# A four-layer graph network on one core: turns between the halves of a product, sorted keys turned in fours, and q rows gathered beside p rows

## The chip, the cores and the metric

The kernel runs on one core of one Trainium2 chip. The metric is the device time of one execution in microseconds (us); the smaller the better. The kernel before takes 6629.94 us, the median of three runs (6616.99 to 6645.70). Beside the times there is one profiled execution with a hardware trace of every engine: TensorE (PE, with its weight loads as PEld), VectorE (DVE), ScalarE (ACT), GpSimd (POOL) and the queue of SyncE (SP).

## What is computed

A graph of 4096 nodes with 512 features and 65,536 edges, sorted by their destination, passes through four layers. Each layer normalizes the nodes, applies a ReLU, runs a graph layer and adds its result to the nodes.

```python
# layer 0: x = x + softmax over the features of an 8-head attention over the edges' distinct pairs
# layer 1: x = x + relu(sum over edges of d[row] * d[col] * h[col], times W1)
# layer 2, h = relu(layernorm(x)):
edge_feat = concatenate([h[src], h[dst], edge_attr], axis=-1)
m = mish(mish(edge_feat @ W1 + b1) @ W2 + b2)          # one message per edge
agg = segment_sum(m, dst, num_segments=4096)
u = mish(concatenate([h, agg], axis=-1) @ W3 + b3)
x = x + layernorm(h + u @ W4 + b4) * gamma + beta
# layer 3: x = x + relu(sum over edges of d[row] * d[col] * (h @ W.T + b)[row])
```

Here mish(x) is x * tanh(softplus(x)). In layer 2 the product of the edge features with W1 is split: p = h @ W1[:512] and q = h @ W1[512:1024] + b1 are made once for each node, kept in two tables in HBM, and an edge's first product is p[src] + q[dst] + edge_attr @ W1[1024:].

## The kernel before

Nodes lie in 32 blocks of 128. Edges are put in order by a sort inside the kernel, and then taken as tiles of 128 edges which all belong to one block of nodes; a tile's sum over its edges is a product with a one-hot matrix.

**The front.** Three pieces of work are written as Python generators and advanced in turn, one step each, by `Side(...).finish()`: `by_order(0)`, the sort of the edges by source node (wrapped in `faster`, which gives it three steps in two rounds); `project`, which makes W0's product for the 32 blocks; and `attributes`, which writes the edge attributes with the edge's ends into a table in HBM. PE, ACT, DVE and POOL execute their instructions in the order in which these steps issue them (`manual_schedule`). So an instruction that has to wait keeps back everything behind it on its engine, from whichever of the three it comes.

A block of `project` is four steps: DVE normalizes it (L547); PE turns it in four transposes into the PSUM tile tr and ACT copies it with a ReLU to h_t (`relu_t`, L424 and L426), and the block before is put away (L531 to L533); two of the four parts of the product (L557); the other two, and then the product for the attention scores (L564). An fp32 matmul of the source is two MATMUL instructions in the trace.

The sort works in place on DVE (L166, L167) and between some of its passes turns all keys with PE and ACT (L174, L176, L178). At its end it fetches each tile's sorted keys with a gather (L276), takes them apart on DVE, and `placed` turns them: five tiles of 128x128, each with one transpose (L288) and one copy by DVE (L289), and one PSUM tile for all. It runs three times for the order by source and once for the order by destination. The latter, `by_order(1)`, is advanced beside the edge loop of layer 1.

**The edge loop of layer 2** (`messages`) takes groups of U2 = 4 tiles, 132 groups in all. It is a software pipeline with the order of each engine written out: at iteration i the rows for group i+2 are fetched, group i+1 gets its attribute products, group i its first mish, group i-1 its second product, and group i-2 its second mish and its sums.

- `fetch_rows` gathers four times 128 rows of p into pg (L452), `add_rows` then gathers the rows of q with an add in the DMA onto the same pg (L1047); `fetch_ends` fetches the attributes and ends (L987). All these are issued by POOL.
- `turn_attributes` (L1061, copied by L1063), then `attribute_products` (L1071), which DVE adds to pg (L1148, L1158).
- The first mish is a Sigmoid, an Arctan and a Sin on ACT into qg (L1118, L1139, L1154), and a product of pg with it on DVE, for the tiles 0 and 1 (L1155) and 2 and 3 (L1163).
- `turn_h` turns a tile of h on PE (L1078) and ACT copies it (L1080). Tiles 0 and 1 of group i are turned at the end of iteration i, among the sums of group i-2; tiles 2 and 3 in iteration i+1 behind the first second product. All turns, with that of the attributes, share two PSUM buffers, tr_ps.
- `second_product` (L441) has two PSUM buffers, m_ps; DVE adds b2 into z (L1121, L1132, L1144, L1161).
- The second mish is on ACT (L1127, L1141, L1150) and DVE (L1152); `add_message` makes the sum of a tile (L1090), and DVE adds it to the block (L462). Attribute products and sums share four PSUM buffers, small_ps.

After the loop the rest of layer 2, and layer 3 with its own edge loop, follow; the change does not touch them.

## Time and profile before

| what | us |
|---|---|
| median of three runs | 6629.94 |
| lowest and highest run | 6616.99, 6645.70 |
| profiled execution, its time | 6629.94 |
| its span, first to last instruction | 6628.1 |
| edge loop of layer 2 | 2926, about 44% of the span |
| front up to the attention loop's first gather | 276 |
| PE busy with second products, L441 m_ps | 1913.9 |
| POOL issuing the adding gathers, L1047 (528 of them) | 939.1 |

The profiled execution is the median run itself; the 1.8 us between its time and its span lie outside the first and last instruction. A row of the timeline gives start, length, engine, line, operation, output and inputs, and how many instructions were merged; in brackets stands how long the engine was idle before the row and which instruction released it. A row's length counts the pipeline of the last matmul, so the starts of neighbouring rows tell more about PE's pace than the lengths. Busy shares over the whole span mix stages; what an edit costs has to be read in its own stage.

### The profile page before, as it was taken

To read this page: it belongs to the slowest core of one execution; us is meant where nothing else is said; L and a number is where in the kernel's file an instruction comes from. 1 tells how busy PE (TensorE), PEld (TensorE's weight loads), DVE (VectorE), ACT (ScalarE), POOL (GpSimd) and SP (SyncE) were. 2 spreads that over 40 slices of the span, in tenths; PEclk is the share of its full clock that TensorE was granted. 3 is DMA by queue.
4 is the path that set the end of the run, shared out by engine and by line. 5 is a ranking of instruction groups with operands and counts; after the bars stand their busy time and mean duration, and the time that the engine had idled before them with its cause. 6 is when DMAs were issued, how large, how long until landed. Compare 5 with 4: busy or idle time off the path is not lost. (4 is left out here: it accounts for less than half of the span.)

```text
span 6628.1 us, 64370 instructions
## 1 busy us (share of the span) xinstructions
PE 5750.5 (87%) x17918; PEld 2937.7 (44%) x17918; DVE 3882.4 (59%) x6892; ACT 3086.4 (47%) x4232; POOL 3658.3 (55%) x3326
## 2 busy tenths in 40 slices
PE   6577777779988789999999999999999999877777
PEld 4356555434443344444444444444444566422222
DVE  7466666836664456565656656565665456545555
ACT  3144444421100167777777777777777533200000
POOL 1255555136666488666676666666666111256665
PEclk9788888889999999999999999999999999977778
DMA  8655555457777555444545554444545211255665
GB/s 228 157 153 155 153 155 154 145 182 221 227 221 204 163 126 114 104 102 102 101 104 103 102 105 101 103 102 103 103 103 104 65 64 67 99 162 168 192 204 162
DMA packets 424655, 908.39 MB, mean 137 GB/s; under 512 B 135734, under 2 KB 135734, under 8 KB 424278
## 3 DMA queue, kind: packets, MB, share of 16 engines
q0 software_dynamic: 264768, 721.66, 43.9%
q1 hardware_dynamic: 159510, 182.40, 8.6%
q8 instruction: 152, 2.49, 0.2%
q14 instruction: 225, 1.84, 0.1%
HBM read 800.88 MB, written 102.94 MB: 136 GB/s over the span
## 5 line engine op out<-in xcount | busy, mean ns | idle before, releaser
L441 PE MATMUL m_ps<-w_sb,h_t 128*128 128x512 f32 x4224 | 1913.9, 596 | 0.2 <-issue 0.2
L846 PE MATMUL sum_ps<-g,oh 128*128 128x512 f32 x2144 | 1158.5, 676 | 272.9 <-DVE acc L462 145.2
L441 PEld LDWEIGHTS m_ps<-w_sb,h_t 128*128 128x128 f32 x4224 | 771.7, 190 | 921.7 <-issue 913.7
L1047 POOL DMA_INDIRECT pg<-qtab,eg x528 | 939.1, 1779 | 160.9 <-issue 158.2
L462 DVE TENSOR_TENSOR acc<-acc,sum_ps 128x512 f32 x800 | 550.1, 688 | 778.5 <-PE sum_ps L846 333.6
L452 POOL DMA_INDIRECT pg<-ptab,eg x528 | 518.5, 982 | 608.0 <-ACT h_t L1080 419.7
L760 PE MATMUL sum_ps<-rows,oh 128*128 128x261 f32 x2176 | 611.0, 435 | 271.8 <-issue 192.7
L846 PEld LDWEIGHTS sum_ps<-g,oh 128*128 128x128 f32 x2144 | 428.8, 212 | 942.8 <-issue 539.7
L452 POOL DMA_INDIRECT g<-ytab,s_dst x544 | 547.1, 1006 | 479.1 <-DMA x_mid<-x 199.1
L452 POOL DMA_INDIRECT rows<-htab,s_dst x544 | 519.9, 956 | 457.1 <-PE sum_ps L760 271.8
L452 POOL DMA_INDIRECT g<-ztab,d_src x528 | 515.9, 977 | 399.1 <-PE sum_ps L846 163.8
L760 PEld LDWEIGHTS sum_ps<-rows,oh 128*128 128x128 f32 x2176 | 445.4, 213 | 374.1 <-issue 208.5
L987 POOL DMA_INDIRECT eg<-aug,d_eid x528 | 508.5, 963 | 161.0 <-issue 159.2
L1080 ACT COPY h_t<-tr_ps 128x512 f32<-128x512 f32 x528 | 296.6, 588 | 562.1 <-PE tr_ps L1078 424.7
L1090 PE MATMUL small_ps<-z,oh 128*128 128x512 f32 x1056 | 533.9, 608 | 8.4 <-DVE z L1152 8.4
L1152 DVE TENSOR_TENSOR z<-z,t 128x1024 f32<-128x1024 f32 x264 | 311.9, 1223 | 207.6 <-issue 185.0
L462 DVE TENSOR_TENSOR acc<-acc,small_ps 128x512 f32 x528 | 362.7, 687 | 87.9 <-DVE acc L462 69.8
L1332 ACT ACTIVATE t_end<-acc,dis 128x512 f32<-128x512 f32 x32 | 23.0, 721 | 835.7 <-DMA g<-ztab,d_src 400.0
L1078 PEld LDWEIGHTS tr_ps<-ident,pg 128*128 128x128 f32 x2112 | 245.9, 141 | 288.0 <-issue 148.2
L1078 PE MATMUL tr_ps<-ident,pg 128*128 128x128 f32 x2112 | 299.5, 275 | 43.9 <-DVE pg L1155 39.6
L1144 DVE TENSOR_TENSOR z<-m_ps,b_bc 128x512 f32<-128x512 f32 x132 | 91.4, 693 | 390.5 <-PE m_ps L441 206.9
L1132 DVE TENSOR_TENSOR z<-m_ps,b_bc 128x512 f32<-128x512 f32 x132 | 91.4, 692 | 374.6 <-PE m_ps L441 371.1
(274 smaller groups left out, 8384.2 us busy)
## 6 DMA issues: line engine op xcount, KB each, us to landing
aug<-row SPq DMA_DIRECT2D x32, 560.0 KB
xt<-in_x_dram SPq DMA_DIRECT2D x16, 1024.0 KB
row<-in_edge_attr_dram SPq DMA_DIRECT2D x32, 512.0 KB
rows<-htab,s_dst POOLq DMA_INDIRECT x544
g<-ytab,s_dst POOLq DMA_INDIRECT x544
eg<-aug,d_eid POOLq DMA_INDIRECT x528
pg<-ptab,eg POOLq DMA_INDIRECT x528
pg<-qtab,eg POOLq DMA_INDIRECT x528
```

The source lines that it names most:

```text
L441: nc.tensor.matmul(ps, h_t[:, k, :], w_sb[:, k0 + k, :], start=start and k == 0, stop=stop and k == KC - 1)
L452: nc.gpsimd.indirect_dma_start(out=dst_ap, out_offset=None, in_=table, in_offset=bass.IndirectOffsetOnAxis(ap=idx, axis=0))
L462: nc.vector.tensor_add(into, into, ps)
L760: nc.tensor.matmul(ps[:, c, :HW], oh[:, j + k, :], rows[:, j + k, c * HW:(c + 1) * HW], start=k == 0, stop=k == 1)
L846: nc.tensor.matmul(ps, oh[:, j + k, :], g[:, j + k, :], start=k == 0, stop=k == pair - 1)
L987: nc.gpsimd.indirect_dma_start(out=eg[:, j // 2, (j % 2) * HALF:(j % 2 + 1) * HALF], out_offset=None, in_=aug.rearrange("e c -> (e c)").un ...
L1047: nc.gpsimd.indirect_dma_start(out=pg[:, j, :], out_offset=None, in_=qtab, in_offset=bass.IndirectOffsetOnAxis(ap=end_of(eg, j, 1), axis=0 ...
L1078: nc.tensor.transpose(h_ps[:, k, :], h[:, j, k * P:(k + 1) * P], ident)
L1080: nc.scalar.copy(h_t, h_ps)
L1090: nc.tensor.matmul(ps, oh, m, start=True, stop=True)
L1132: nc.vector.tensor_add(zz[:, 1, :], ps, b2_bc)
L1152: nc.vector.tensor_mul(mz[:, j:j + 2], mz[:, j:j + 2], t[:, j:j + 2])
```

## The change

It has three parts.

In `project` the normalizing moves into a generator `norms` that hands out blocks. A block's turn is issued between the first and the second half of the product of the block in front of it; before its own product come that second half and the score product.

In `placed` four tiles are turned into one PSUM tile and copied with one DVE instruction, then the fifth; a step ends between transposes and copy, and work of the other generators is issued there.

In the edge loop the rows of q are gathered into a tile of their own, qg, with three buffers, and DVE adds them to pg in two instructions. The same tile then takes the Sigmoid. Tiles 0 and 1 of a group are turned at the beginning of the next iteration, directly before its first second product, and no longer among the sums; the turn of the attributes follows directly on those of tiles 2 and 3; the attribute products come before the third second product and no longer after it; `fetch_ends` is issued before `fetch_rows`. DVE's product for tiles 2 and 3 moves behind the second sum.

```diff
         def placed(into, what):
-            for g in range(G):
-                n = min(P, TT - g * P)
-                ps = ppool.tile([P, P], F32, name="turn")
-                nc.tensor.transpose(ps, what[:, g, :], ident)
-                nc.vector.tensor_copy(into[:, g * P:g * P + n], ps[:, :n])
+            for g in range(0, G, 4):
+                n = min(4, G - g)
+                ps = ppool.tile([P, n, P], F32, name="turn")
+                for k in range(n):
+                    nc.tensor.transpose(ps[:, k, :], what[:, g + k, :], ident)
+                yield
+                cols = slice(g * P, min((g + n) * P, TT))
+                nc.vector.tensor_copy(into[:, cols], ps.rearrange("p g t -> p (g t)")[:, :cols.stop - cols.start])
...
-            placed(d_eid, val)
+            yield from placed(d_eid, val)
...
-                yield
-                h_t = relu_t(lp, lps, hn)
-                if waiting is not None:
-                    put_away(*waiting)
-                yield
-                ps = lps.tile([P, D], F32, name="wh_ps")
-                for k in range(KC):
-                    nc.tensor.matmul(ps, h_t[:, k, :], w_sb[:, k, :], start=k == 0, stop=k == KC - 1)
-                    if k == 1:
-                        yield
...
+        h_t = relu_t(lp, lps, hn)
+        hn = next(made)
+        yield
         waiting = None
+        for b in range(NB):
+            ps = lps.tile([P, D], F32, name="wh_ps")
+            for k in range(KC // 2):
+                nc.tensor.matmul(ps, h_t[:, k, :], w_sb[:, k, :], start=k == 0, stop=False)
+            yield
+            h_next = relu_t(lp, lps, hn) if b + 1 < NB else None
+            if waiting is not None:
+                put_away(*waiting)
+            yield
+            for k in range(KC // 2, KC):
+                nc.tensor.matmul(ps, h_t[:, k, :], w_sb[:, k, :], start=False, stop=k == KC - 1)
+            hn = next(made, None)
+            yield
...
             def fetch_rows(eg):
                 pg = lp.tile([P, U2, D], F32, name="pg", bufs=4)
+                qg = lp.tile([P, U2, D], F32, name="qg", bufs=3)
                 for j in range(U2):
                     gather(pg[:, j, :], ptab, end_of(eg, j, 0))
-                return pg
-
-            def add_rows(eg, pg):
-                for j in range(U2):
-                    nc.gpsimd.indirect_dma_start(
-                        out=pg[:, j, :], out_offset=None, in_=qtab,
-                        in_offset=bass.IndirectOffsetOnAxis(ap=end_of(eg, j, 1), axis=0), compute_op=OP.add)
+                    gather(qg[:, j, :], qtab, end_of(eg, j, 1))
+                return pg, qg
...
             for i in range(-3, NG + 2):
                 now = lambda k: 0 <= k < NG
-                if now(i + 2):
-                    rows[i + 2] = fetch_rows(fetched[i + 2])
                 if now(i + 3) and i + 3 not in fetched:
                     fetched[i + 3] = fetch_ends(first, i + 3, ends_pool)
                 if now(i + 2):
-                    add_rows(fetched[i + 2], rows[i + 2])
+                    rows[i + 2] = fetch_rows(fetched[i + 2])
                 if now(i - 1):
                     hh = h.pop(i - 1)
                     zz = z[i - 1] = lp.tile([P, U2, D], F32, name="z", bufs=2)
+                    h_t = [turn_h(0, hh), turn_h(1, hh)]
                 if now(i):
-                    pg = h[i] = rows.pop(i)
-                    qg = lp.tile([P, U2, D], F32, name="qg", bufs=2)
+                    pg, qg = rows.pop(i)
+                    h[i] = pg
                     nc.scalar.activation(qg, pg, AF.Sigmoid, scale=-1.0)
                 if now(i - 1):
-                    ps = second_product(h_t.pop(0))
+                    ps = second_product(h_t[0])
                     nc.vector.tensor_add(zz[:, 0, :], ps, b2_bc)
-                    h_t[2], h_t[3] = turn_h(2, hh), turn_h(3, hh)
+                    h_t += [turn_h(2, hh), turn_h(3, hh)]
+                if now(i + 1):
+                    et = turn_attributes(fetched[i + 1])
+                    nxt, nxt_q = rows[i + 1]
...
-                if now(i + 1):
-                    et = turn_attributes(fetched.pop(i + 1))
-                    nxt = rows[i + 1]
                 if i == 0:
                     first_mish(pg, qg)
+                if now(i + 1):
+                    made = attribute_products(et)
+                    for j in range(2):
+                        nc.vector.tensor_add(nxt[:, j], nxt[:, j], made[j])
+                    nc.vector.tensor_add(nxt[:, :2], nxt[:, :2], nxt_q[:, :2])
...
                 if now(i - 1):
-                    ps = second_product(h_t.pop(2))
+                    ps = second_product(h_t[2])
+                if now(i + 1):
+                    for j in range(2, U2):
+                        nc.vector.tensor_add(nxt[:, j], nxt[:, j], made[j])
+                    nc.vector.tensor_add(nxt[:, 2:], nxt[:, 2:], nxt_q[:, 2:])
+                if now(i - 1):
                     nc.vector.tensor_add(zz[:, 2, :], ps, b2_bc)
-                if now(i + 1):
-                    made = attribute_products(et)
-                    for j in range(2):
-                        nc.vector.tensor_add(nxt[:, j], nxt[:, j], made[j])
...
-                if now(i + 1):
-                    for j in range(2, U2):
-                        nc.vector.tensor_add(nxt[:, j], nxt[:, j], made[j])
                 if now(i - 1):
-                    ps = second_product(h_t.pop(3))
+                    ps = second_product(h_t[3])
                     nc.vector.tensor_add(zz[:, 3, :], ps, b2_bc)
-                if now(i) and i > 0:
-                    nc.vector.tensor_mul(pg[:, 2:], pg[:, 2:], qg[:, 2:])
                 for j in range(U2):
-                    if now(i) and j >= 2:
-                        h_t[j - 2] = turn_h(j - 2, pg)
                     if now(i - 2):
                         add_message(first + (i - 2) * U2 + j, oh[:, j, :], mz[:, j, :])
+                    if now(i) and i > 0 and j == 1:
+                        nc.vector.tensor_mul(pg[:, 2:], pg[:, 2:], qg[:, 2:])
```

## The prediction

> **What bounds the kernel now.** I read the page's busy shares first, then a table by stage, then the PE rows in order of time in the two stages that the change touches.
>
> ```profile
> PE 5750.5 (87%) x17918; PEld 2937.7 (44%) x17918; DVE 3882.4 (59%) x6892; ACT 3086.4 (47%) x4232; POOL 3658.3 (55%) x3326
> ```
>
> ```profile
> 47.00:209.00 162.00, 141.78 (x605) 83.96 (x605) 124.70 (x367) 46.12 (x102) 10.45 (x36) 0.99 0.83 221
> ...
> 231.00:250.00 19.00, 6.83 (x16) 3.02 (x17) 9.95 (x25) 0.00 (x0) 1.63 (x9) 0.63 1.03 278
> 250.00:266.00 16.00, 13.86 (x52) 7.53 (x50) 1.62 (x7) 2.73 (x5) 0.00 (x0) 0.91 0.18 70
> 2317.00:5243.00 2926.00, 2858.64 (x8711) 1312.79 (x8711) 1742.24 (x2503) 2172.91 (x1721) 1954.18 (x1572) 0.99 0.49 103
> ```
>
> The second fence is the table by stage (length, then PE, PEld, DVE, ACT, POOL busy, granted clock, DMA share, GB/s). The Layer 2 edge loop is 2926 us, 44% of the span, with PE busy 98% of it and DVE 60%: PE paces it. The sort beside the projection (47 to 209) has PE at 88% and DVE at 77%. From 231 to 250 PE does almost nothing.
>
> ```profile
> 4503.46 3.70 PE L441 MATMUL m_ps<-w_sb,h_t 128*128 128x512 f32 x8
> 4506.99 1.88 PE L1090 MATMUL small_ps<-z,oh 128*128 128x512 f32 x4
> 4509.18 0.63 PE L1078 MATMUL tr_ps<-ident,pg 128*128 128x128 f32 x4 [0.31 <-DVE pg L1155]
> 4509.69 1.13 PE L1090 MATMUL small_ps<-z,oh 128*128 128x512 f32 x2
> 4510.65 0.60 PE L1078 MATMUL tr_ps<-ident,pg 128*128 128x128 f32 x4
> 4511.09 1.02 PE L1090 MATMUL small_ps<-z,oh 128*128 128x512 f32 x2
> 4511.95 3.60 PE L441 MATMUL m_ps<-w_sb,h_t 128*128 128x512 f32 x8
> 4515.38 1.04 PE L1078 MATMUL tr_ps<-ident,pg 128*128 128x128 f32 x8
> 4516.26 3.60 PE L441 MATMUL m_ps<-w_sb,h_t 128*128 128x512 f32 x8
> 4519.69 0.38 PE L1061 MATMUL tr_ps<-ident,eg 128*128 128x128 f32 x2
> 4519.91 3.60 PE L441 MATMUL m_ps<-w_sb,h_t 128*128 128x512 f32 x8
> 4523.44 1.13 PE L1071 MATMUL small_ps<-w1e,et 64*128 64x512 f32 x4
> ```
>
> This is one iteration in the timeline of PE. I call the four second products P0 to P3, the turns of their h tiles T0 to T3, the attribute turn E, the four attribute products A, the messages M0 to M3. P0 starts 21.90 us after the P0 before it (the Sigmoid rows of ACT, L1118, stand 21.90 apart in four places of the loop). From start to start: a product 3.43, a turn 0.43, E 0.22, A 1.72, a message 0.86; four, four, one, one and four of them make 20.82 us. The other 1.08 is what a better order could win at most: 0.47 before T0, which waits for DVE's L1155, and some 0.1 at each of six changes of kind or restarts (a product after A or after a wait takes 3.53 to the next row, not 3.43).
>
> ```profile
> 4511.29 0.59 ACT L1080 COPY h_t<-tr_ps 128x512 f32<-128x512 f32 x1 [0.85 <-PE tr_ps L1078]
> 4511.89 1.28 ACT L1118 ACT_TABLE_LOAD   x1
> ...
> 4516.02 1.07 ACT L1080 COPY h_t<-tr_ps 128x512 f32<-128x512 f32 x2 [0.92 <-PE tr_ps L1078]
> ```
>
> A copy starts 0.64 after its turn's first row (4515.38 to 4516.02) and takes 0.59. Now in the front:
>
> ```profile
> 190.54 0.63 PE L424 MATMUL tr<-ident,hn 128*128 128x128 f32 x4
> 191.87 3.70 PE L557 MATMUL wh_ps<-w_sb,h_t 128*128 128x512 f32 x8 [0.69 <-ACT h_t L426]
> 195.40 0.96 PE L564 MATMUL s_ps<-wa,h_t 128*128 128x16 f32 x8
> ```
>
> A product that needs the turn just ahead of it starts 1.33 after that turn, 0.90 later than the turn's own 0.43, and then needs 3.53.
>
> [...] L1152 of the same shape measures 1223. [...] the Sigmoid starts 1.30 after the load's start (4511.89 to 4513.19), so I use 1.30.
>
> **Part 1, the edge loop.** Removed: 4 adding gathers of 1.78 us on POOL (L1047), and T0, T1 from among the messages. Added: 4 plain gathers (0.98, as L452) and two DVE adds of 1.22. Moved: T0 and T1 to the iteration's start, directly ahead of P0; E from behind P1 to directly behind T3; A from behind P2 to behind P1. New PE order: T0 T1 P0 T2 T3 E P1 A P2 P3 M0 M1 M2 M3.
>
> Walked from T0 = 0. Its copy ends at 0.64 + 0.59 = 1.23 and P0 starts at 1.33, not 0.86. P0 restarts, so T2 at 4.86. ACT copies twice (to 1.7), then load and Sigmoid (1.30 + 1.91) to 4.9: free. The tr_ps pool has two buffers, so E needs T2's, which is free when its copy ends at 4.86 + 1.23 = 6.09; E starts at 6.15 instead of 5.72. With a restart of 0.08, P1 at 6.45. Then A 9.98 (3.53), P2 11.90 (1.92), P3 15.43 (3.53 behind A), M0 18.86, next T0 22.40 (3.44 and 0.10). That is 0.50 more than 21.90: about 0.57 at P0 and 0.50 at E come, and the wait on L1155 with its restart and one change of kind, about 0.6, go.
>
> DVE beside it: A's first results at 9.98 + 1.16 (4501.54 to L1148 at 4502.70), two adds, the first new add, two adds, the second new add, at 0.60 and 1.14 apiece: 15.8; the z add behind P2 to 16.5; z times t, two of 1.14, to 17.6 and 18.8 (the Sin on t ends at 15.9: E's copy ends at 7.0, then on ACT a Sigmoid and two Arctans of 1.9, a load of 1.3, the Sin); pg times qg to 19.9. M0 needs 17.6 and comes at 18.9; the next T0 needs 19.9 and comes at 22.4. So the adds are covered, with 1.2 us to spare; beyond that each us would cost 132. POOL goes from 18.5 us (4 x (0.96 + 0.98 + 1.78) + 12 x 0.30) to 15.2. The qg buffers, three, come free with L1184 some 23 us into the iteration; the rows are needed about 31 us later, and seven gathers at 1.27 plus landing fit. DVE and ACT rows queue behind no new wait longer than that. Queue behind the waiting P0 and E: all of PE, and through it DVE's z adds, which have 2 us or more.
>
> 132 x 0.50 = 66 us more. Bounds: no restart cost and P0 and E at the very end of the copies, 22.08, +24; each wait 0.15 longer (the front's later turns: 253.75 to 255.13 and 259.48 to 261.13 are 1.38 and 1.65), 22.7, +106. First fill: 8 gathers of 1.27 in place of 4 and 4 longer ones, 3 us less.
>
> **Part 2, the projection.** Now T of the next block lies between the halves of a product, so the 0.90 and the restart 0.1 per block can go. But DVE's 124.7 of 162 us are nearly as tight: 26 blocks in 161.8 us (first rows of L557 at 47.23 and 208.99), 6.22 each, of which PE's own work is 3.43 + 0.81 + 0.43 + some 0.25 for the sort's turns, 4.9, and DVE's 4.8. Neither reaches its sum, since each sort turn hands the key from DVE to PE to ACT and back. I take 0.6 of a possible 1.3, 16 us; bounds 5 and 26.
>
> **Part 3, sorted keys.** Five round trips of 0.72 to 0.86 three times (233.6 to 249.8) become two, of about 1.6 and 0.8: some 4 us. Two product halves and one score row go in between, and two and a half blocks behind (249.6 to 265.6) become less than two: about 7 us. Steps yielded in the sort let the others advance; SP's and POOL's attribute loads move with them, with DMA at 1.03 of its share there, so I count 8 of these 11. In Layer 1 four round trips of 0.86 (2044.16 to 2047.0) become one: 3 us. Bounds for both: 4 and 15.
>
> **Sum.** 6628.1 + 66 - 3 - 16 - 8 - 3 = 6664, and 1.8 outside the span: 6666. The profiled execution is the median run itself, 6629.94; the runs lie from 6617 to 6646.
>
> **Rivals.** *The adds bind.* Against: 1.2 us to spare. For: DVE rises to 15.7 of 22.4 us, and the messages stand behind six DVE instructions that start only with A. If DVE is late by 0.5 beyond its slack, another 66: 6732. *The waits are cheaper.* If the loop's two waits cost together 0.7 instead of 1.08, the loop is 16 longer, the rest wins its 30, and the total is 6616: no change that can be told. *Faster.* T0's freed wait is the larger effect in the loop, and the front pays fully (26 + 15 + the fill's 3). With both new waits together at 0.5 the loop would be at 21.82, 11 us less, and the total 6575. With the front as summed it decides where both waits together fall below 0.55. Against: the same turn, copy and product take 1.33 in the front at the loop's own clock. That the q rows come late I leave out: POOL has 7 us to spare in each iteration.
>
> **Numbers.** Two waits as walked 0.56, the adds bind 0.14, cheaper waits 0.20, faster 0.10. About 0.5%, 33 us, is what a measurement of this kernel can tell from no change. The likeliest case, at 6666, lies just above that line, so 0.10 of its 0.56 falls below: slower 0.46 + 0.14 = 0.60, same 0.10 + 0.20 = 0.30, faster 0.10. Range: 6624 (loop +24, the rest 30 less) to 6717 (loop +106, the rest 19 less); what the adds' case has above it, and the two cheaper cases below it, are left out.
>
> **What would show it.** In the changed trace PE rows P0 and E each carry a wait of some 0.4 us for ACT's h_t copy, T0 waits for nobody, P0 to P0 is 22.4, and the rows on DVE's new adds have no DMA wait. In the front the product halves carry no ACT wait, and the first Layer 0 gather, at 276 now, starts near 250. I am wrong if M0 waits for DVE, if E does not wait, or if the projection stays at 6.2 us a block.

## The result, and the profile after

The changed kernel takes 6799.20 us, the median of four runs (6791.16 to 6812.83); the kernel before takes 6637.82 on the same chip (four runs, 6616.99 to 6651.72). The ratio is 1.0248, 95% interval 1.0212 to 1.0284: slower by about 161 us, where 6666 (36 more than before) was forecast. The direction was right and the size was far too small: the time lies above the range.

The profiled execution has a span of 6811.0 us, 182.9 more than before. Cut at the first instruction of each stage, the two traces differ like this:

| stage, first instruction to the next stage's first | before, us | after, us | difference |
|---|---|---|---|
| front, to the first Layer 0 gather | 276.0 | 262.9 | -13.1 |
| attention loop of Layer 0 | 993.8 | 1023.0 | +29.2 |
| products of Layer 1 | 142.8 | 143.7 | +0.9 |
| edge loop of Layer 1 | 906.6 | 902.8 | -3.8 |
| edge loop of Layer 2 | 2928.7 | 3090.6 | +161.9 |
| rest of Layer 2 | 527.8 | 528.3 | +0.5 |
| Layer 3 | 852.4 | 859.7 | +7.3 |

Almost everything is in the edge loop of Layer 2. The page of the changed kernel has these groups there (busy us and mean ns of one, then the idle time of the engine just before and what ended it):

```profile
PE 5778.7 (85%) x17918; PEld 2964.0 (44%) x17918; DVE 4180.5 (61%) x7144; ACT 3071.7 (45%) x4232; POOL 3320.9 (49%) x3326
...
L444 PE MATMUL m_ps<-w_sb,h_t 128*128 128x512 f32 x4224 | 1909.2, 600 | 31.2 <-ACT h_t L1096 31.2
...
L455 POOL DMA_INDIRECT qg<-qtab,eg x528 | 500.5, 948 | 1048.2 <-ACT h_t L1096 883.6
...
L1007 POOL DMA_INDIRECT eg<-aug,d_eid x528 | 588.9, 1115 | 161.0 <-issue 125.0
...
L1106 PE MATMUL small_ps<-z,oh 128*128 128x512 f32 x1056 | 482.9, 600 | 89.3 <-DVE z L1173 88.5
```

The second products (L444) now wait 31.2 us in all for ACT's copies; that was forecast. The sums of the messages (L1106) wait 88.5 us for DVE's product of z with t; that was named as a sign that the forecast is wrong. DVE's busy time is up by 298 us and POOL's down by 337.

Two iterations of PE's timeline show where both waits stand:

```profile
4494.77 1.04 PE L1094 MATMUL tr_ps<-ident,pg 128*128 128x128 f32 x8
4496.04 3.70 PE L444 MATMUL m_ps<-w_sb,h_t 128*128 128x512 f32 x8 [0.24 <-ACT h_t L1096]
4499.58 1.04 PE L1094 MATMUL tr_ps<-ident,pg 128*128 128x128 f32 x8
4500.85 0.44 PE L1077 MATMUL tr_ps<-ident,eg 128*128 128x128 f32 x2 [0.24 <-ACT h_t L1096]
4501.13 3.60 PE L444 MATMUL m_ps<-w_sb,h_t 128*128 128x512 f32 x8
4504.66 1.99 PE L1087 MATMUL small_ps<-w1e,et 64*128 64x512 f32 x8
4506.57 7.13 PE L444 MATMUL m_ps<-w_sb,h_t 128*128 128x512 f32 x16
4513.55 3.60 PE L1106 MATMUL small_ps<-z,oh 128*128 128x512 f32 x8
4516.98 1.04 PE L1094 MATMUL tr_ps<-ident,pg 128*128 128x128 f32 x8
...
4528.79 7.13 PE L444 MATMUL m_ps<-w_sb,h_t 128*128 128x512 f32 x16
4537.45 3.70 PE L1106 MATMUL small_ps<-z,oh 128*128 128x512 f32 x8 [1.53 <-DVE z L1173]
```

The first iteration, from T0 at 4494.77 to the next T0 at 4516.98, is 22.21 us: P0 starts 1.27 after T0 and E 1.27 after T2, where the two turns alone take 0.86, and nothing else waits. The second has the same order up to P2 and P3 at 4528.79, but its first sum stands 1.53 us idle, and the iteration takes 24.0. Such iterations alternate with the others through nearly the whole loop. DVE in the same two iterations:

```profile
4509.59 1.22 DVE L1167 TENSOR_TENSOR pg<-pg,qg 128x1024 f32<-128x1024 f32 x1
4510.73 0.68 DVE L1169 TENSOR_TENSOR z<-m_ps,b_bc 128x512 f32<-128x512 f32 x1
4511.33 2.35 DVE L1173 TENSOR_TENSOR z<-z,t 128x1024 f32<-128x1024 f32 x2
...
4531.80 1.22 DVE L1167 TENSOR_TENSOR pg<-pg,qg 128x1024 f32<-128x1024 f32 x1
4535.58 0.69 DVE L1169 TENSOR_TENSOR z<-m_ps,b_bc 128x512 f32<-128x512 f32 x1 [2.55 <-remote]
4536.18 2.35 DVE L1173 TENSOR_TENSOR z<-z,t 128x1024 f32<-128x1024 f32 x2
```

L1169 adds b2 to the result of P2, and waits for nothing but P2. In both iterations P2's last matmul has started by then (4509.68 and 4531.90) and takes 0.6. In the first, L1169 follows L1167 without a gap. In the second, P2 is done by 4532.5, L1167 by 4533.0, and L1169 starts at 4535.58. "remote" says that a semaphore for which L1169 waits was updated just then, and that the profile finds no instruction that ended there. The trace's records of these updates tell more: it is PE's semaphore. Ahead of every late add of this trace an update of it is recorded 22 to 24 ns before the add starts, and 1.6 to 3.3 us (median 3.1) after the end of P2's last matmul. In rows_by_sp, dma_add and the runs on chip D (all below) it is recorded 13 to 15 ns after that end. So DVE goes on as soon as PE's signal is there; it is the signal that comes late. I call this a late z add. From 2700 to 5100 us the trace holds 104 of these adds (some records are missing); 51 are late, by 0.9 to 2.7 us. Behind a late one stand the products of z with t, and M0 waits for the first of these.

### The profile page after: what moved, and what is told of

Same layout as the page of the kernel before. It is cut to its first block, busy times and chain, and to the rows that moved or that the text cites. A ratio compares the mean times of both kernels' runs of the same rounds, so it can differ in the third digit from the quotient of the medians.

```text
span 6811.0 us, 65003 instructions
## 1 busy us (share of the span) xinstructions
PE 5778.7 (85%) x17918; PEld 2964.0 (44%) x17918; DVE 4180.5 (61%) x7144; ACT 3071.7 (45%) x4232; POOL 3320.9 (49%) x3326
## 5 line engine op out<-in xcount | busy, mean ns | idle before, releaser
L444 PE MATMUL m_ps<-w_sb,h_t 128*128 128x512 f32 x4224 | 1909.2, 600 | 31.2 <-ACT h_t L1096 31.2
L866 PE MATMUL sum_ps<-g,oh 128*128 128x512 f32 x2144 | 1142.4, 669 | 294.7 <-DVE acc L465 159.4
L444 PEld LDWEIGHTS m_ps<-w_sb,h_t 128*128 128x128 f32 x4224 | 772.4, 190 | 986.5 <-issue 837.9
L455 POOL DMA_INDIRECT qg<-qtab,eg x528 | 500.5, 948 | 1048.2 <-ACT h_t L1096 883.6
L1007 POOL DMA_INDIRECT eg<-aug,d_eid x528 | 588.9, 1115 | 161.0 <-issue 125.0
L455 POOL DMA_INDIRECT pg<-ptab,eg x528 | 552.9, 1047 | 221.3 <-issue 160.4
L1106 PE MATMUL small_ps<-z,oh 128*128 128x512 f32 x1056 | 482.9, 600 | 89.3 <-DVE z L1173 88.5
L1150 DVE TENSOR_TENSOR z<-m_ps,b_bc 128x512 f32<-128x512 f32 x132 | 91.3, 692 | 480.4 <-issue 397.8
L1106 PEld LDWEIGHTS small_ps<-z,oh 128*128 128x128 f32 x1056 | 196.1, 190 | 364.9 <-issue 212.1
L787 DVE TENSOR_TENSOR acc<-acc,sum_ps 128x522 f32 x272 | 189.5, 697 | 176.4 <-PE sum_ps L780 161.5
```

What stands on the lines that cost most here:

```text
L444: nc.tensor.matmul(ps, h_t[:, k, :], w_sb[:, k0 + k, :], start=start and k == 0, stop=stop and k == KC - 1)
L455: nc.gpsimd.indirect_dma_start(out=dst_ap, out_offset=None, in_=table, in_offset=bass.IndirectOffsetOnAxis(ap=idx, axis=0))
L787: nc.vector.tensor_add(into, into, ps[:, :, :HW])
L866: nc.tensor.matmul(ps, oh[:, j + k, :], g[:, j + k, :], start=k == 0, stop=k == pair - 1)
L1007: nc.gpsimd.indirect_dma_start(out=eg[:, j // 2, (j % 2) * HALF:(j % 2 + 1) * HALF], out_offset=None, in_=aug.rearrange("e c -> (e c)").un ...
L1106: nc.tensor.matmul(ps, oh, m, start=True, stop=True)
```

## Experiments

The kernels ran on five chips beside the kernel before, so ratios are compared, and stage times come from each run's own trace. "Mean" is the mean of 80 iterations in the middle of the loop, "late" the share of late z adds behind P2 (starting over 0.2 us after the end of P2 and of DVE's instruction before), "clock" the granted clock over the execution.

| kernel | chip | clock | ratio to before, 95% | Layer 2 loop, us | mean | late |
|---|---|---|---|---|---|---|
| before | | 0.930 | 1 | 2928.7 | 21.90 | |
| after | | 0.929 | 1.0248 (1.0212 to 1.0284) | 3090.6 | 23.05 | 51 of 104 |
| front_only | A | 0.921 | 0.9971 (0.9959 to 0.9983) | 2928.9 | 21.90 | |
| loop_only | A | 0.921 | 1.0316 (1.0281 to 1.0352) | 3125.0 | 23.24 | 44 of 103 |
| add_late | A | 0.922 | 1.0095 (1.0059 to 1.0131) | 2988.7 | 22.22 | 6 of 108 |
| rows_first | A | 0.920 | 1.0285 (1.0256 to 1.0313) | 3122.9 | 23.31 | 47 of 103 |
| turn_after_sum | B | 0.931 | 1.0059 (1.0041 to 1.0078) | 2985.0 | 22.34 | |
| turns_back | B | 0.926 | 1.0013 (0.9995 to 1.0032) | 2922.8 | 21.71 | 1 of 110 |
| rows_by_sp | B | 0.927 | 1.0061 (1.0045 to 1.0078) | 2963.6 | 22.22 | 0 of 108 |
| dma_add | B | 0.930 | 1.0036 (1.0023 to 1.0050) | 2974.3 | 22.22 | 0 of 108 |
| adds_together | C | 0.928 | 0.9847 (0.9827 to 0.9867) | 2850.0 | 21.26 | |
| ends_apart | C | 0.927 | 0.9908 (0.9877 to 0.9940) | 2860.9 | 21.26 | 13 of 113 |
| no_adds | C | 0.927 | 1.0275 (1.0235 to 1.0316) | 3098.0 | 23.09 | 99 of 104 |
| after_again | C | 0.929 | 1.0254 (1.0237 to 1.0271) | 3091.8 | 23.08 | 52 of 104 |
| p_then_q | D | 0.980 | 1.0029 (1.0019 to 1.0040) | 2968.3 | 22.21 | 0 of 99 |
| no_q_gathers | D | 0.979 | 1.0013 (1.0006 to 1.0020) | 2963.1 | 22.22 | 0 of 99 |
| ends_by_sp | D | 0.979 | 1.0020 (1.0010 to 1.0031) | 2968.4 | 22.21 | 0 of 100 |
| before_again | D | 0.977 | one run | 2928.8 | 21.90 | |
| after_third | E | 0.929 | 1.0261 (1.0231 to 1.0290) | 3090.1 | 23.07 | 49 of 104 |
| p_then_q_2 | E | 0.930 | 1.0249 (1.0219 to 1.0279) | 3110.8 | 23.11 | 49 of 104 |

My theory A was that DVE's late instruction costs time because the two q adds ate the slack ahead of M0; the rival B, that the waits for ACT's copies are all of it. Both, and the expectations below, speak of a stall of DVE where the semaphores' records show a late signal.

**front_only**: the functions of the front as changed, the edge loop's as before.

> Front and sorted keys as changed, the Layer 2 edge loop as before. In the changed trace the first Layer 0 gather is 13.1 us earlier (262.9 against 276.0), the attention loop then takes 29 us longer (first row of y_ps minus first gather: 1023.0 against 993.8) and layer 1 is 4 shorter. If the longer attention loop belongs to the new front: about 6638 - 13 + 29 - 4 = 6650. If it is an accident of that execution, or comes from elsewhere: 6638 - 17 = 6621. The Layer 2 loop itself stays at 2929 us and 21.90 an iteration under every theory.

Ratio 0.9971, some 20 us gained, and the loop is 2928.9 us. The attention loop took 1101.5, but loop_only, with the old front on the same chip, took 1122.5. So the front gains, and on this chip the attention loop is not longer with it.

**loop_only**: the reverse.

> Front as before, the Layer 2 edge loop as changed. If the loop's loss is its own (3090.5 against 2928.7 us): 6638 + 162 = 6800. If it depends on what the new front leaves behind: nearer to 6638 + 66 = 6704. The attention loop tells the same from the other side: 994 us if its loss belongs to the new front, 1023 if it is an accident.

The loop alone carries the loss (3125.0 us), on this chip even a little more than in the first trace.

**add_late**:

```diff
                     for j in range(2, U2):
                         nc.vector.tensor_add(nxt[:, j], nxt[:, j], made[j])
-                    nc.vector.tensor_add(nxt[:, 2:], nxt[:, 2:], nxt_q[:, 2:])
...
                     if now(i) and i > 0 and j == 1:
                         nc.vector.tensor_mul(pg[:, 2:], pg[:, 2:], qg[:, 2:])
+                    if now(i + 1) and j == 2:
+                        nc.vector.tensor_add(nxt[:, 2:], nxt[:, 2:], nxt_q[:, 2:])
```

> As changed, but DVE's second q add (L1167) is moved behind the third sum, so that the z add L1169 and the products of z with t stand 1.22 us earlier on DVE. Theory A, every second iteration DVE stalls for some 1.6 to 2.6 us just before L1169 and the adds have eaten the slack that would hide it: with 1.2 us more slack most of the stall is hidden, iterations go from 22.2 and 24.1 in turn to 22.2 and at most 22.9, and the time falls by 66 x 1.2 to 66 x 1.9 = 80 to 125, to 6675 to 6720. Theory B, the loss is in the waits for ACT's copies at P0 and E alone: no change, 6799.

Of the 80 iterations in the middle 77 take 22.2, and against loop_only on the same chip 136 us of the loop are gone. B falls. DVE in this kernel's timeline:

```profile
4505.34 1.28 DVE L1166 TENSOR_TENSOR pg<-pg,small_ps 128x512 f32<-128x512 f32 x2
4507.37 0.69 DVE L1168 TENSOR_TENSOR z<-m_ps,b_bc 128x512 f32<-128x512 f32 x1 [0.75 <-PE m_ps L444]
4507.98 2.35 DVE L1172 TENSOR_TENSOR z<-z,t 128x1024 f32<-128x1024 f32 x2
```

The reader sees that the stall is not hidden here, as A had it: it is not there. DVE stands 0.75 us and goes on the moment P2 ends. Only 6 of 108 z adds are late. With the DVE add moved, PE's signal comes in time; why, the traces do not say.

**rows_first**:

```diff
+                if now(i + 2):
+                    rows[i + 2] = fetch_rows(fetched[i + 2])
                 if now(i + 3) and i + 3 not in fetched:
                     fetched[i + 3] = fetch_ends(first, i + 3, ends_pool)
-                if now(i + 2):
-                    rows[i + 2] = fetch_rows(fetched[i + 2])
```

> As changed, but the rows are fetched before the ends again, so that on POOL the four gathers of ends no longer stand ahead of the first gather of p rows. In the changed trace every stall of DVE before L1169 begins as POOL issues that first p gather, 0 to 0.1 us before L1167 ends or while it runs. If that gather's issue holds DVE up, its moving takes the stall away: all iterations 22.2, about 6675. If DVE stalls by itself, or POOL's order does not matter: 24.1 every second time as now, 6799. If the rows now come too late for DVE's adds: waits for a DMA at L1157 or L1167, slower than 6799.

No change from loop_only. It could tell little: gathers of rows and of ends follow each other in a circle, so the ends still stand ahead of the next p gather on POOL.

**turn_after_sum**: an attempt at a faster loop. From front_only:

```diff
                 for j in range(U2):
-                    if now(i) and j >= 2:
-                        h_t[j - 2] = turn_h(j - 2, pg)
                     if now(i - 2):
                         add_message(first + (i - 2) * U2 + j, oh[:, j, :], mz[:, j, :])
+                    if now(i) and j >= 2:
+                        h_t[j - 2] = turn_h(j - 2, pg)
```

> Front and sorted keys as changed, the Layer 2 edge loop as before but for one swap: the turns of tiles 0 and 1 stand behind the sums of tiles 2 and 3 instead of ahead of them. Before, PE waits 0.31 us for DVE's L1155 at T0 (0.47 with the restart). With T0 one sum (0.86) later L1155 is done, and P0 follows T0 by 0.43 + 0.86 + 0.43 = 1.72, more than the 1.33 that turn, copy and product take. If that wait is removable: 21.90 - 0.47 = 21.43 an iteration, 132 x 0.47 = 62 us less than front_only, ratio about 0.988. If ACT's chain from the attribute turn to the Sin paces the loop: 21.90 stays, ratio 0.997. If the later copies hold up ACT's Sigmoid: longer than 21.90.

A miss: 22.34 an iteration.

```profile
4510.16 1.88 PE L1110 MATMUL small_ps<-z,oh 128*128 128x512 f32 x4
4512.85 1.12 PE L1110 MATMUL small_ps<-z,oh 128*128 128x512 f32 x2 [0.81 <-DVE pg L1178]
4513.82 0.60 PE L1098 MATMUL tr_ps<-ident,pg 128*128 128x128 f32 x4
```

T0 (4513.82) no longer waits, but M2 (4512.85) now waits 0.81 for DVE's L1178, the add that frees the PSUM buffer which M2 writes. In the kernel before, T0's own wait probably covered that one; no run shows it apart.

**turns_back**: add_late without `h_t = [turn_h(0, hh), turn_h(1, hh)]` at the iteration's start, and at the end of each of the last two sums:

```diff
+                    if now(i) and j >= 2:
+                        turned_h.append(turn_h(j - 2, pg))
```

> As add_late, but with the turns of tiles 0 and 1 back among the sums, behind the sums of tiles 2 and 3, and no longer directly ahead of P0. In add_late's trace P0 starts 1.27 after T0 where the two turns alone take 0.86. If P0's wait for the copy costs these 0.41: 21.80 instead of 22.21 an iteration, 54 us less than add_late, ratio near 1.001. If T0 then has to wait for DVE's L1176, or the wait is only moved: 22.2, ratio 1.0095.

The wait at P0 costs 0.50 an iteration (22.22 to 21.71): the 0.41 that starts show, and a remainder of some 0.1, about what the prediction took for a restart.

**rows_by_sp**:

```diff
-                    gather(pg[:, j, :], ptab, end_of(eg, j, 0))
-                    gather(qg[:, j, :], qtab, end_of(eg, j, 1))
+                    r = fetches[0] % NB * P
+                    nc.sync.dma_start(pg[:, j, :], ptab[r:r + P, :])
+                    nc.sync.dma_start(qg[:, j, :], qtab[r:r + P, :])
+                    fetches[0] += 1
```

> As changed, but the rows of p and q are not gathered by POOL: SP's queue fetches 128 consecutive rows of each table, so every edge gets the rows of wrong nodes; all adds and products stay, and as many bytes are moved. POOL issues only the four gathers of ends in an iteration. If DVE's stalls come from POOL issuing gathers while DVE works on SBUF: no idle time before L1169 and between the adds beyond what PE explains, all iterations 22.2, loop about 2990 us. If DVE stalls by itself in this order of instructions: 22.2 and about 24 in turn as in the changed kernel, loop 3090 to 3120.

**dma_add**:

```diff
-                    gather(qg[:, j, :], qtab, end_of(eg, j, 1))
+                for j in range(U2):
+                    nc.gpsimd.indirect_dma_start(
+                        out=pg[:, j, :], out_offset=None, in_=qtab,
+                        in_offset=bass.IndirectOffsetOnAxis(ap=end_of(eg, j, 1), axis=0), compute_op=OP.add)
...
-                    nc.vector.tensor_add(nxt[:, :2], nxt[:, :2], nxt_q[:, :2])
...
-                    nc.vector.tensor_add(nxt[:, 2:], nxt[:, 2:], nxt_q[:, 2:])
```

> As changed in every order, but the q rows are added by the gather as before the change, and DVE's two q adds are left away. It prices the order alone. If the two waits for ACT's copies are the whole cost of the order: 22.21 - 21.90 = 0.31 an iteration, 41 us, all iterations alike, with front_only's gain a ratio of 0.9971 + 0.0062 = 1.003. If the stalls come with the order of PE and not with the adds: 22.2 and 24 in turn, ratio about 1.025. If the longer issue of adding gathers on POOL (1.78 against 0.95) holds something up that the changed kernel does not: between the two.

Both have 22.22 in every iteration and no late z add. So the new order of PE by itself costs 0.32 an iteration. About the late add neither is proof: the changed kernel was not run on chip B.

**adds_together**: from turn_after_sum:

```diff
                     made = attribute_products(et)
-                    for j in range(2):
+                    for j in range(U2):
                         nc.vector.tensor_add(nxt[:, j], nxt[:, j], made[j])
...
-                if now(i + 1):
-                    for j in range(2, U2):
-                        nc.vector.tensor_add(nxt[:, j], nxt[:, j], made[j])
```

> As turn_after_sum (front and sorted keys as changed, loop as before with the turns of tiles 0 and 1 behind the sums of tiles 2 and 3), and DVE's four adds of attribute products stand together, ahead of the products of z with t. In turn_after_sum PE waits 0.81 us at the sum of tile 2 for DVE, whose adds for tiles 2 and 3, which free the PSUM buffer that this sum writes, stand behind L1178. DVE is idle 1.55 us before the products of z, and two adds take 1.2, so the move costs nothing. If so the wait goes and the first one at T0 does not come back: 21.3 to 21.45 an iteration, 60 to 80 us less than front_only, ratio 0.985 to 0.988. If ACT's chain paces the loop: 21.90, ratio 0.997.

21.26 an iteration and 0.9847 (0.9827 to 0.9867): faster than both kernels, by about 102 us of 6657 against before. PE's timeline:

```profile
4500.15 2.74 PE L1110 MATMUL small_ps<-z,oh 128*128 128x512 f32 x6
4502.73 0.60 PE L1098 MATMUL tr_ps<-ident,pg 128*128 128x128 f32 x4
4503.16 1.02 PE L1110 MATMUL small_ps<-z,oh 128*128 128x512 f32 x2
4504.02 0.60 PE L1098 MATMUL tr_ps<-ident,pg 128*128 128x128 f32 x4
4504.46 3.60 PE L444 MATMUL m_ps<-w_sb,h_t 128*128 128x512 f32 x8
4507.90 1.04 PE L1098 MATMUL tr_ps<-ident,pg 128*128 128x128 f32 x8
```

M0 to M2, T0, M3, T1 and P0 carry no bracket: neither of the two waits of before and of turn_after_sum is left. The new front is in it, the q adds are not.

**ends_apart**: turns_back with the turn of the attributes in a PSUM buffer of small_ps.

```diff
-                et_ps = lps.tile([P, U2 // 2, P], F32, name="tr_ps")
+                et_ps = lps.tile([P, D], F32, name="small_ps", bufs=4)[:, :U2 // 2 * P].rearrange(
+                    "p (j t) -> p j t", j=U2 // 2)
```

> As turns_back, but the turn of the attributes is written to a buffer of small_ps instead of tr_ps, so that it no longer waits until ACT has copied the turn of tile 2. In turns_back it starts 1.27 after that turn where the two turns alone take 0.86. If that wait is what it costs: 21.71 - 0.41 = 21.30 an iteration, 54 us less than turns_back, ratio about 0.993. If the five buffers' worth of work in four of small_ps makes a sum or an attribute product wait for DVE instead: 21.7 or more, ratio 1.001 or more.

E's wait is worth 0.45 (21.71 to 21.26). With both waits gone the changed kernel's scheme is as fast an iteration as adds_together's.

**no_adds**: the two lines with nxt_q are left away; the gathers stay.

> As changed, but DVE's two q adds are left out: the q rows are gathered as in the changed kernel and used by nobody, so the first products lack q. If the adds take the slack that would hide DVE's stall: 22.2 in every iteration, loop about 2975, as in dma_add. Outside the loop, kernels with q rows in a tile of their own have so far been 16 to 35 us longer by their ratio than loop and front explain, in the attention loop for the most part; dma_add and turn_after_sum have not. If the gathers or the tile bring that, it stays: ratio near 1.007. If the adds bring it: ratio 1.003 to 1.004, as dma_add.

This was the surprise, and it takes theory A down: without any q add the kernel is as slow as with them (1.0275 beside 1.0254 of after_again on the same chip), and 99 of 104 z adds are late.

```profile
3468.11 1.28 DVE L1165 TENSOR_TENSOR pg<-pg,small_ps 128x512 f32<-128x512 f32 x2
3475.18 0.69 DVE L1167 TENSOR_TENSOR z<-m_ps,b_bc 128x512 f32<-128x512 f32 x1 [5.79 <-PE m_ps L444]
3475.79 2.35 DVE L1171 TENSOR_TENSOR z<-z,t 128x1024 f32<-128x1024 f32 x2
```

The last matmul of P2 started at 3470.78 here, so the add is 3.8 us late. DVE has nothing else to do for 5.79 us. Here too an update of PE's semaphore, the first recorded since P2's end, stands 0.02 us ahead of the add's start. Giving DVE slack does not help while it waits for a signal that comes late.

**after_again**: the changed kernel.

> The changed kernel itself, beside these three on one chip. Ratio 1.025 as before; iterations of 22.2 and about 24 in turn; attention loop 15 to 35 us longer than in adds_together's trace from the same chip if that belongs to the kernel, no fixed difference if it is an accident.

1.0254, as the first time. The attention loops were 1022.0 us in adds_together and 1030.5 here.

**p_then_q**:

```diff
                     gather(pg[:, j, :], ptab, end_of(eg, j, 0))
+                for j in range(U2):
                     gather(qg[:, j, :], qtab, end_of(eg, j, 1))
```

> As changed, but POOL gathers the four rows tiles of p first and then the four of q, instead of p and q in turn. In the changed trace DVE's z add behind P2 is late in every iteration in which POOL issues the first p gather of a group just then (51 of 51), and in none in which POOL is still at the gathers of ends (0 of 53). Behind that p gather POOL then stands for the q buffer. If it is the p gather as such: late as often, about 23.1 an iteration in the mean. If it is POOL's standing for the q buffer behind it: with four p gathers ahead of that wait the add is late less, and the mean falls towards 22.2.

**no_q_gathers**: the line with qtab left away, and nxt in place of nxt_q in the two adds.

> As changed, but the q rows are not gathered: DVE's two adds add the p tile to itself, so q is left out and p counted twice. DVE's instructions, their order and their lengths stay; POOL issues 8 gathers an iteration instead of 12. no_adds has shown iterations of 23.1 in the mean without DVE's adds. If the gathers make DVE's z add late: 22.2 in every iteration here, loop about 2975. If the adds make it late after all: 22.2 and 24 in turn, loop 3090. Outside the loop all kernels without adding gathers were some 25 us longer than loop and front explain; if it is their absence, that stays here: ratio about 1.007; if it is q's gathers into a tile of their own: 1.004.

**ends_by_sp**:

```diff
-            nc.gpsimd.indirect_dma_start(
...
-                in_offset=bass.IndirectOffsetOnAxis(ap=d_eid[:, t:t + 1], axis=1))
+            r = t % (E // P) * P
+            nc.sync.dma_start(eg[:, j // 2, (j % 2) * HALF:(j % 2 + 1) * HALF], aug[r:r + P, j % 2 * 3:j % 2 * 3 + HALF])
```

> As changed, but the ends and attributes of the edges are fetched by SP's queue from consecutive rows, so tiles get the ends of wrong edges; POOL issues only the 8 gathers of rows, which it ends some 5 us earlier in an iteration. If the late z add needs POOL to issue a gather of rows at that time: 22.2 in every iteration, loop about 2975. If it comes with the plain gathers of rows whenever they are issued: still 23 in the mean, loop 3090.

**before_again**: the kernel before.

> The kernel before itself, for its stages beside those of the other three on one chip: 21.90 an iteration and 2929 us for the loop. If the attention loop's extra 16 to 36 us in kernels without adding gathers belong to them, it is that much shorter here than in p_then_q, no_q_gathers and ends_by_sp; if they are accidents, no fixed difference.

None of the three has a late z add, and all have 22.2 in every iteration. But the chip was another kind: granted clock 0.98 over the execution, and even the kernel before takes 6115.54 us there, with an attention loop of 724.2. So the changed kernel and p_then_q went together to one more chip.

**after_third** and **p_then_q_2**: the changed kernel and p_then_q.

> The changed kernel a third time, because p_then_q, no_q_gathers and ends_by_sp ran on a chip whose granted clock is 0.98 over the execution instead of 0.92 to 0.93, and none of them had a late z add there. If this chip is of that kind too: with 22.2 in every iteration and a ratio near 1.003 the late add belongs to the chips with the lower clock, and those three say nothing of its cause; with 22.2 and 24 in turn and a ratio near 1.027 (163 of 6115) each of the three took the cause away. On a chip with 0.93: 1.025 as before.

> As p_then_q, beside the changed kernel on one chip. If the order of POOL's gathers decides: no late z add, 22.2 in every iteration, some 120 us less than after_third. If it was the chip: the same iterations as after_third, whichever these are.

On this chip p_then_q has the late adds as the changed kernel has (49 of 104 in both), at the places where the same kernel had none on chip D. So the order of POOL's gathers does not decide, and the three runs on chip D say nothing about the cause.

**What is settled and what is open.** Shown in the traces: a late z add waits for PE's signal, and the signal comes late. Shown on one chip each: the late z add goes with the changed loop, not with the front (front_only, loop_only); it does not need the q adds (no_adds beside after_again); it is all but gone when the second q add stands behind the third sum (add_late beside loop_only and rows_first; ends_apart, which keeps that order, beside after_again). Shown across chips: one and the same kernel has it on one chip and not on another.

Late signals are not new with the change. In the attention loop the reduction L725 on DVE reads a product of PE's L719. This is the kernel before on the first chip:

```profile
332.15 0.36 PE L719 MATMUL e_ps<-of,oh_t 128*128 128x48 bf16 x8
...
335.12 0.56 DVE L725 TENSOR_REDUCE near<-e_ps 128x128 f32<-128x384 f32 x1 [2.70 <-PE sum_ps L760]
```

And the same kernel on chip D (before_again):

```profile
425.29 0.36 PE L719 MATMUL e_ps<-of,oh_t 128*128 128x48 bf16 x8
...
425.69 0.56 DVE L725 TENSOR_REDUCE near<-e_ps 128x128 f32<-128x384 f32 x1
```

The bracket names a sum of PE, but the update that starts L725 is recorded 0.7 us after that sum's end and belongs to no recorded end. The longest such wait in this trace is 23.4 us: five updates of PE's semaphore are recorded one after another from 320.75 to 320.92, while PE's last product had ended at 302.6. It looks as if updates were held back and then let through in a row. In the kernel before, 64 of 68 such reductions on the first chip start over 0.2 us late in this way (median 2.3 us), on chip D none. In all, DVE stands idle 183 us ahead of these late ones in the attention loop of 993.8 us, 201 in the changed kernel's of 1023.0, 257 to 277 in those of 1101 to 1126 on chip A, and 0 in those of 719 to 724 on chip D.

What makes PE's signal late is open. In the changed kernel's first trace POOL was issuing the first p gather of a group in all 51 late cases and the gathers of ends in all 53 others, but in p_then_q_2 that p gather stood beside late and punctual adds alike, and in no_adds 91 of the 99 late ones stood beside gathers of ends. One rival is untested: the recording of the trace itself. On chip D the traces hold every update of a semaphore by PE, DVE and ACT within 0.1 us of its instruction's end; on the other chips many records are missing (p_then_q: 23,879 updates from 2700 to 5000 us on chip D, 10,757 on chip E), the most in the kernels with many late adds. No execution here is known to have run without that recording.

## Why the prediction was wrong

By its own terms, with the iterations' sums (131 intervals of the first Sigmoid: 2857.7 before, 3022.4 after; 2899 to 2900 in rows_by_sp, no_q_gathers, ends_by_sp and p_then_q, which keep the changed order on PE and have no late adds):

| term | forecast | measured |
|---|---|---|
| waits at P0 and E, less T0's | +66 | +42 |
| late z adds | 0 | +123 |
| first fill and drain of the loop | -3 | -3 |
| projection and sorted keys, to the first gather | -24 | -13 in this trace, about -20 in front_only's ratio |
| sorted keys in Layer 1 | -3 | -4, within what this stage varies by |
| attention loop and Layer 3, untouched | 0 | +36.5 in this trace |

- *The walk of the iteration was right.* P0 1.27 behind T0 (1.33 forecast), E 1.27 behind T2 (1.29), the sums 18.78 after T0 (18.86), no wait at T0, none for a DMA at the new adds. The sum came to 22.21 instead of 22.40; 0.10 of the difference is a restart at the next T0, which isn't there (3.43 from M0 to T0). Both new waits measured 0.95 together (0.50 and 0.45), where 1.07 was taken, and what they replace was worth 0.64 (0.95 - 0.31), not 0.6.
- *The step that failed is "So the adds are covered, with 1.2 us to spare".* The DVE times in it hold: the z add ends 16.6 after T0 in an undisturbed iteration (16.5 forecast), the first product of z 17.8 (17.6). The new adds (L1157, L1167) take 1.22 to 1.23 us, as L1152 of the same 128x1024 shape did before the change (1223 ns in the mean). What failed is that the z add was taken to start as soon as P2 had ended and DVE was free. PE's signal of that end comes 1.6 to 3.3 us late in every second iteration (51 of 104). The z add then starts 0.9 to 2.7 us later than the walk has it, more than the 1.2 in all but 6 cases, and M0 is late by the rest: 123 us over the loop, a term that the sum had at nothing. Why the signal is late stays open.
- *The rival "the adds bind" had the place right and the cause wrong.* Its sign, M0 waiting for DVE, is what the trace shows, and its 6732 was the nearest of the cases; but no_adds shows that it is not the adds' work. That it came nearest is luck. (The range's upper end takes 19 us off outside the loop, where the lower bounds given there, 5, 4 and 3, make 12; 6724 would have missed as well.)
- *The front was right in kind.* Between 47 and 209 us the halves of a product carry no wait for ACT; L557 had 44.8 us of it in the kernel before. The 26 blocks took 154.0 us in place of 161.8, 8 of the 16 us taken. One block of 13.12 us takes much of the rest:

```profile
70.02 0.96 PE L588 MATMUL s_ps<-wa,h_t 128*128 128x16 f32 x8
76.79 2.08 PE L176 MATMUL turn<-turns,key 128*128 128x128 f32 x8 [5.81 <-DVE key L167]
78.66 3.34 PE L574 MATMUL wh_ps<-w_sb,h_t 128*128 128x512 f32 x4
81.84 0.60 PE L427 MATMUL tr<-ident,hn 128*128 128x128 f32 x4
82.28 1.88 PE L581 MATMUL wh_ps<-w_sb,h_t 128*128 128x512 f32 x4
```

  PE stands 5.81 us for a key, and the half product after it takes 3.34 us, the next one 1.88. The clock records have half speed from 74.8 to 81.6 here, beginning 3.8 us into that stand (the granted clock from 75 to 81 is 0.50); in the kernel before they have none from 51.5 to 218.7. Issuing a sort's turn ahead of a product makes the product wait with it. The first gather came at 262.9, not near 250: the turns of the sorted keys end at 244.1 instead of 249.8, but they start at 229.0 instead of 233.6, so they themselves gained 1.1 us where 4 were forecast. What stands behind them up to the first gather took 18.8 us instead of 26.2, about the 7 that were forecast.
- *The attention loop* is untouched by the change. Of its 29 us, 18 are idle time of DVE ahead of late signals (201 us in place of 183), and PE was at half clock for 330 us of it in this trace and for 297 before. On the chips tried it took 719 to 1126 us, and pairs on one chip differed by up to 36. By their ratios, loop_only, add_late, rows_first, rows_by_sp, turns_back, ends_apart, no_adds and after_again are some 18 to 35 us longer than loop and front explain, dma_add, turn_after_sum and adds_together are not, and nothing of it shows on chip D; why stays open.

## What to carry to other kernels

A slack worked out from instruction durations is the most there can be, not what there is: when a change moves the bound engine's next instruction behind a longer chain on another engine, let the forecast's range hold what a few us of late start on that chain cost in every iteration. The trace of before can tell how large that is: compare, wherever one engine waits for another, the start with the end of what it waited for (2.3 us at L725 here). Ahead of the work that PE waits for, put only what that work needs: moving one DVE instruction behind the third sum brought back two thirds of the loss on chip A (ratio 1.0095, beside 1.0285 in rows_first). Look first for waits that stand directly on the pacing engine: two reorderings that took 0.3 us and 0.8 us waits off PE gave 1.2%, more than new buffers and gathers did.

## What the runs showed of the hardware that was not expected

- The signal by which PE tells DVE of a finished product can come late: 1.6 to 3.3 us after the product's end in 51 of 104 iterations of the changed kernel, up to 3.8 us in no_adds, against 13 to 15 ns in dma_add, rows_by_sp and on chip D. The same program (p_then_q) had late adds in 49 of 104 cases on one chip and in 0 of 99 on another. Whether the recording of the trace plays a part is not known.
- Chips differ more than the change does: 6115.54 us for the kernel before on chip D and 6776.66 on chip A. Most of it lies where PE often waits: its attention loop took 724.2 us on chip D, with 52 us at half clock and no late signal at L725, and 993.8 on the first chip, with 297 at half clock and 183 us of DVE idle ahead of late signals. The edge loop of Layer 2, where PE is busy throughout, took 2928.8 and 2928.7 us.
- POOL's gathers of ends took 1115 ns in the mean after the change (page line above) and 963 before. From 2700 to 5100 us of the changed kernel, the 264 gathers whose issue began while DVE worked on a 128x1024 instruction took up to 2.0 us (median 1.40), the 988 others 0.94 to 1.09. On DVE's side nothing is seen: the 247 such instructions that started during a gather's issue took 1.21 to 1.23 us, as all others did. Why the gathers are longer there is not shown, and no run here ties the late z add to it.
